# Unit steps in order with values by row tiles, projections in the turned tokens' place, the last diagonal ahead of its index search

## The chip, the cores and the metric

The kernel runs on one core of a Trainium2 chip. Times are device microseconds from the first to the last work of one execution. The engines have these names in the profile: PE is TensorE (PEld its weight loads), DVE VectorE, ACT ScalarE, POOL GpSimd, SP SyncE, whose queue issues most DMA transfers. L12 means line 12 of the kernel before.

## The reference

The block is a "macaron": half an expert layer, attention, half an expert layer, each on a normalised input and added to it. x has 8 batches of 1024 tokens of 512 values; there are 32 experts, each takes 8 tokens of a batch.

```python
def ffn(x):                                   # _layernorm(x) goes in
    logits = einsum('bsd,ed->bse', x, gate_w) + gate_b
    probs = softmax(logits, axis=-2)          # over the tokens
    vals, idx = top_k(probs by expert, 8)
    tok = x[idx];  merged = sum_k(tok * vals) # one mixed token per expert and batch
    h = gelu([merged, 1] @ w1[e]);  o = [h, 1] @ w2[e]
    return scatter_add(o * vals at idx)
def attn(x):                                  # 16 heads of 32
    q, k, v = split_heads(x @ Wq.T + bq), ...
    q = exp(q);  k = exp(k)
    kv = cumsum(k[:, :, :, None] * v[:, :, None, :], axis=1);  k1 = cumsum(k, axis=1)
    out = einsum('zsD,zsDd->zsd', q, kv) / sum(q * k1)
    return merge(out) @ Wo.T + bo
x = x + 0.5 * ffn(layernorm(x))
x = x + attn(layernorm(x))
x = x + 0.5 * ffn(layernorm(x))
```

## The kernel before

The work has four stretches.

**Prologue (0 to about 130 us).** For each batch `gate` (L1335 on) loads and normalises x, turns the tokens (rT, from the pool `rp` of four buffers) and multiplies them with the gate weights; `finish` scales the logits. `choose` (L398 on) takes the eight largest of each expert with MAX8, MATCH_REPLACE8 and FIND_INDEX8; `gather_four` (L431) multiplies the chosen weights with the tokens of four batches (ps_pmT, ps_m). Meanwhile SP's queue loads the first tiles of expert weights (w<-in_w, 2 MB each, named w1_i_e_n and w2_i_e_n). When the pools of the prologue close, new pools are opened on the right side of memory for the projections, and `load_projections` (L200) loads wo, wq, wk and wv, 1 MB each. From wo come ps_bo (L1431), the turned wo (ps_woT) and its product with the gate weights (ps_woG).

**First experts (to about 828 us).** `experts` multiplies each expert's weights with the mixed tokens (h_ps L1206, p_ps L1229). Since this waits for the weights, `speculate` (L1074) runs between: for batches 4 to 7 it computes the q, k and v projections of the input before the expert layer was added and writes them to memory (`ahead_d`), without the scale of the normalisation.

**Attention (to about 1960 us).** Eight batches, each in 8 chunks of 128 tokens; two chunks make a unit (U=2). The loop over b and c (L983 to L1061) gives the order of PE by hand, and the scheduler places what is not pinned (`keep_in_program_order`) on the other engines by its own costs. A chunk runs: `scores` (sp L766, then the mask: am0 on DVE L777, am1 on ACT L782 and selects on POOL L784), in an even chunk `denominators` (ps_den L728, its reciprocal rd L736), then a step of the generator `ahead` (which prepares the next unit), `turn_keys` (ps_kt L816, kc), `project_out` of the chunk before (ps_o L880, addition to xt L887), in an even chunk `spread_denominators` (ps_rr L747), a step of `gate` (the second gate, routed batch by batch) and `attend` (ps_n L830 and L842, at L851, the running sum ps_kv L862 to kv). `begin` adds the first expert layer's result to a later batch's tokens (`scatter_two`, ps_sc L293 and L300, xt L308).

For batches 0 to 3 the generator is `project`. For batches 4 to 7 it is `project_rest` (L619), in steps that `yield` separates. In an even chunk: bo is added to xt (POOL L631), the token scales are spread (ps_rs L636, rsb), pmr (POOL L646) is the routing weight times scale, and pre, the loaded projections, is multiplied by the scale (POOL L650, two halves). In an odd chunk, behind project_out: ps_qk (L663) adds the expert layer's part as a product of pmr and oW; un is its sum with pre (two additions on DVE, L672), and eight exps on ACT (L675); `sum_keys` runs the scan over the keys on DVE (L709, four groups of heads og); ps_v (L684), for each chunk of the unit a product of pmr with oWv, and va (DVE L688); `times_keys` multiplies q and k1 on POOL (qk L720), which the next unit's ps_den reads. pmr holds the same 32 rows four times over (pm4); both ps_v products read the same rows r, those of the batch.

**Last gate and second experts (to the end).** The last batch's gate is done in parts of 4, 2, 1 and 1 chunks (`route` L486). Its last part: the token scales are turned (ps_rsT L378), copied to rsT by ACT (L380), spread (ps_rs L387), the logits scaled, then `choose`, pinned in order with FIND_INDEX8 last (L427), then diag (L512), ps_pmT (L519), pmT, ps_m (L539) and ps_mT (L562). SP waits for ps_m before it can load a next weight tile, as the memory is shared.

Of the kernel before, what the change touches and what calls it, by code (L numbers as in the profile page):

```python
# [15 lines left out]
P = 128  # L16
# [4 lines left out]
def kernel(  # L21
# [188 lines left out]
    def open_token_pools(stack: ExitStack, attention: bool, early=None, keep=None) -> Token:  # L210
        t = Token()
        if attention:


            t.un = keep.enter_context(tc.tile_pool(name="un", bufs=1))
            t.xp = keep.enter_context(tc.tile_pool(name="xp", bufs=1, reuse_waits="tile"))
            t.a1 = stack.enter_context(tc.tile_pool(name="a1", bufs=1))
            t.a2 = stack.enter_context(tc.tile_pool(name="a2", bufs=2))
            t.ow = stack.enter_context(tc.tile_pool(name="ow", bufs=1))
            t.n2 = early.enter_context(tc.tile_pool(name="n2", bufs=2, side="right"))  # L220
        if not attention:
# [150 lines left out]
    def gate_scale(t, s, b, lg, rs, at, k):  # L372
# [6 lines left out]
        rsT = t.p2.tile([NCH, P], F32, tag="rsT", name=f"rsT_{b}_{at}")  # L379
        nc.scalar.copy(rsT[:k, :], pr[:k, :])  # L380
        yield
# [21 lines left out]
    def choose(t, lg, rows, g, name, listed=False, el=None):  # L403
# [21 lines left out]
        if pinned:  # L425
            tc.keep_in_program_order(
                nc.vector.max_index(chosen_idx[rows, g, :], top[rows, :], lg[rows, :])  # L427
            )
        return rest, sm[rows, 2:3]
# [51 lines left out]
    def route(t, s, b, el=None):  # L481
# [30 lines left out]
        nc.vector.tensor_scalar_mul(diag[rows, :], ident[rows, rows], r)  # L512
        if el is None:
# [105 lines left out]
    def project_rest(t, s, b, u):  # L619

        xt, mv, rs = s["xt", b]
        pre = s.pop(("pre", b, u))
# [30 lines left out]
        yield  # L653
        yield

# [17 lines left out]
        for n, bias in ((1, bk_sb), (0, bq_sb)):  # L673
            for oc in range(NDC):
                nc.scalar.activation(  # L675
                    qkT[:, oc, n, :], qkT[:, oc, n, :], AF.Exp, bias=bias[:, oc : oc + 1]
                )
        sum_keys(t, s, b, u)

        r = slice(32 * (b % 4), 32 * (b % 4) + E)  # L680
        for i in range(U):
            c = u * U + i
            ps = t.mm.tile([P, D], F32, tag="mm", name=f"ps_v_{b}_{c}")
            nc.tensor.matmul(  # L684
                ps, lhsT=pmr[r, i * P : (i + 1) * P], rhs=s["oWv"][r, :], start=True, stop=True
            )
            va = t.a2.tile([P, D], F32, tag="va", bufs=3, name=f"va_{b}_{c}")
            nc.vector.scalar_tensor_tensor(  # L688
                va,
                pre[:, (2 * NDC + i * 2) * UT : (2 * NDC + i * 2 + 2) * UT],  # L690
                rs[:, c : c + 1],
                ps,
                ALU.mult,
                ALU.add,
            )
            s["va", b, c] = va
        times_keys(t, s, b, u)
        yield

# [4 lines left out]

    def sum_keys(t, s, b, u):
        k1 = s["k1", b, u]
        before = s.pop(("k1", b, u - 1), None)
        for og in range(NDC):
            nc.vector.tensor_tensor_scan(  # L709
                k1[:, og, :],  # L710
                ones.to_broadcast([P, UT]),
                s["k", b, u][:, og, :],
                0.0 if before is None else before[:, og, UT - 1 : UT],
                ALU.mult,
                ALU.add,
            )

    def times_keys(t, s, b, u):
        qk = t.a1.tile([P, NDC, UT], F32, tag="qk", name=f"qk_{b}_{u}")
        nc.gpsimd.tensor_mul(qk, s["q", b, u], s["k1", b, u])  # L720
        s["qk", b, u] = qk
# [189 lines left out]
    def outputs_ahead(t, s):  # L911
# [4 lines left out]
        for i in range(2):  # L916
# [13 lines left out]
            evacuate(s["oW"][:, 2 * i : 2 * i + 2], ps)  # L930
        s["oWv"] = t.ow.tile([P, D], F32, name="oWv")
# [5 lines left out]
        evacuate(s["oWv"], ps)  # L937

    def attention(t, early, preload):
# [47 lines left out]
        for b in range(B):  # L987
            for c in range(NCH):
                if c == 0:
# [15 lines left out]
                if c > 1:  # L1005
                    next(begun, None)
                if b == B - 1 and c == 1:
                    preload(0)
                if b == B - 1 and c == NCH - 2:
# [6 lines left out]
                    )  # L1016
                    gate = route(t, s, b, el)
                scores(t, s, b, c)
                if c % U == 0:
                    denominators(t, s, b, c // U)  # L1020
                    nb, nu = divmod(b * (NCH // U) + c // U + 1, NCH // U)
                    if (nb, nu) == (NB0, 0):
# [9 lines left out]
                        )  # L1032
                        load_ahead(t, s, nb, nu)
                    if (nb, nu) > (0, 1):
                        of = project if nb < NB0 else project_rest
# [255 lines left out]
    with ExitStack() as stack:  # L1291
        big = stack.enter_context(tc.tile_pool(name="big0", bufs=1))
        with ExitStack() as inner:
# [10 lines left out]
            ]  # L1304
            t = open_token_pools(inner, False)
            (
# [322 lines left out]
```

## Time and profile before

| what | value |
|---|---|
| median of 3 runs | 2622.33 us (2621.52 to 2624.72) |
| the profiled execution | 2632.39 us, its span 2630.6 us |
| PE busy, share | 2192.9 us, 83% |
| DVE, ACT, POOL busy | 869.0, 500.2, 376.7 us |
| DMA moved | 667.98 MB, 254 GB/s over the span |
| mean granted clock of TensorE | 0.910 |
| 830 to 1495 us (batches 0 to 3) | PE 648.33 of 665 us, clock 0.99, 30 GB/s |
| 1515.8 to 1631 us (batch 4) | PE 104.93 of 115.2 us, clock 0.88 |
| 1631 to 1747 us (batch 5) | PE 101.83 of 116 us, clock 0.91 |
| 1747 to 1863 us (batch 6) | PE 104.15 of 116 us, clock 0.85 |
| 1863 to 1961 us (batch 7) | PE 87.79 of 98 us, clock 0.95 |

The page's second part shows the span in 40 equal slices: a digit is the busy share in tenths (9 is 90% or more), PEclk the clock granted to TensorE in tenths of full speed, DMA the busy share of the 16 DMA engines. A line of waits says which operation of an engine waited for which operation of another, how long in all, how often, and the longest. A timeline line gives start, duration, engine, line and operation, and in square brackets the idle time before it with what ended it. Granted clock 0.5 means that matmuls take twice the time, which a busy share does not show.

### The profile page before, as it was taken

How to read it: one execution, taken by the hardware profiler on the slowest of the kernel's cores; microseconds unless marked ns; L12 is line 12 of the kernel's file. 1: busy time of each engine (PE TensorE's matmuls, PEld its weight loads, DVE VectorE, ACT ScalarE, POOL GpSimd, SP SyncE). 2: the span in 40 equal slices, each digit the busy share in tenths (PEclk: the TensorE clock that was granted, in tenths of full speed). 3: DMA queues.
4: the chain of work that ended last, by engine and by line, in shares of the span. 5: the costliest groups of instructions: out<-in, count | busy, mean ns of one | idle time of the engine just before them, and what ended most of it. 6: DMA issues, size and time to landing. Idle time of an engine off the chain costs nothing.

```text
span 2630.6 us, 41801 instructions
## 1 busy us (share of the span) xinstructions
PE 2192.9 (83%) x18679; PEld 1161.7 (44%) x18679; DVE 869.0 (33%) x1493; ACT 500.2 (19%) x967; POOL 376.7 (14%) x345
## 2 busy tenths in 40 slices
PE   8699999998986999999999989898886656656555
PEld 5354445444533666666666655555541111111111
DVE  7311111111101443444535476767651000100002
ACT  6310000000000322222222243343430000000000
POOL 0000000000000212111122244444324000000002
PEclk9899999999997999999999988988997787777887
DMA  7699999999996000010100323323149999999995
GB/s 275 253 427 426 428 427 427 426 427 427 428 429 255 1 17 1 21 49 19 58 2 19 91 86 129 118 99 107 66 175 377 423 427 428 428 428 428 428 428 248
DMA packets 95477, 667.98 MB, mean 254 GB/s; under 512 B 18222, under 2 KB 22574, under 8 KB 58432
## 3 DMA queue, kind: packets, MB, share of 16 engines
q1 hardware_dynamic: 73792, 621.45, 57.4%
q10 hardware_dynamic: 18432, 35.66, 3.5%
q0 software_dynamic: 3072, 8.19, 0.8%
q8 instruction: 147, 2.41, 0.4%
q14 instruction: 34, 0.28, 0.0%
HBM read 614.34 MB, written 48.23 MB: 252 GB/s over the span
## 4 chain that ended last, share of the span: by engine, by line
PE 49%; issue 22%; DMA 18%; DVE 7%; ACT 3%; POOL 1%; SPq 0%; ACTq 0%; POOLq 0%; DVEq 0%
DMA w<-in_w 13%; PE ps_o L880 8%; PE ps_k L599 4%; PE ps_q L599 4%; PE ps_v L800 4%; PE ps_sk L1116 3%; PE ps_sq L1116 2%; PE p_ps L1229 2%; PE ps_n L830 2%; PE sp L766 2%; PE h_ps L1206 2%; PE ps_sv L1133 2%; PE ps_n L842 2%; DMA pg<-pmT_d,chosen_idx 1%; DVE st L314 1%
## 5 line engine op out<-in xcount | busy, mean ns | idle before, releaser
L1206 PE MATMUL h_ps<-w,mT 128*8 128x512 f32 x2048 | 287.1, 696 | 120.3 <-DMA w<-in_w 118.3
L1229 PE MATMUL p_ps<-w,pm 128*32 128x512 f32 x1024 | 177.9, 830 | 137.3 <-DMA w<-in_w 133.9
L1215 DVE STREAM_TRANSPOSE hs<-h_ps 128x512 f32<-128x512 f32 x64 | 45.9, 717 | 719.2 <-PE h_ps L1206 719.2
L880 PE MATMUL ps_o<-wo_sb,at 128*128 128x512 f32 x512 | 240.0, 613 | 0.9 <-DVE at L851 0.8
L1206 PEld LDWEIGHTS h_ps<-w,mT 128*8 128x8 f32 x2048 | 50.9, 95 | 338.2 <-issue 206.9
L1229 PE MATMUL p_ps<-w,gl 128*32 128x512 f32 x1024 | 135.1, 658 | 41.9 <-DMA w<-in_w 40.0
L590 POOL TENSOR_TENSOR xt<-xt,bo_sb 128x512 f32<-128x512 f32 x32 | 45.8, 1446 | 798.0 <-PE ps_ocT L338 737.9
L1229 PEld LDWEIGHTS p_ps<-w,pm 128*32 128x32 f32 x1024 | 35.7, 132 | 276.6 <-issue 130.8
L880 PEld LDWEIGHTS ps_o<-wo_sb,at 128*128 128x128 f32 x512 | 96.2, 198 | 101.9 <-issue 98.1
L784 POOL TENSOR_SCALAR_AFFINE_SELECT am<-am 128x512 f32<-128x512 f32 x128 | 78.7, 639 | 414.3 <-ACT am L782 272.3
L314 DVE BATCH_NORM_STATS2 st<-xt 128x6 f32<-128x512 f32 x192 | 129.3, 685 | 4.9 <-DMA xt<-in_x 2.0
L599 PE MATMUL ps_k<-xnT,wk_sb 128*128 128x256 f32 x512 | 115.3, 383 | 10.8 <-ACT xnT L339 10.8
L1222 ACT ACTIVATE pm<-a 128x128 f32<-128x128 f32 x32 | 9.9, 309 | 588.5 <-DVE a L1217 588.5
L1116 PE MATMUL ps_sq<-xcT,wq_sb 128*128 128x256 f32 x512 | 117.9, 387 | 4.0 <-ACT xcT L241 4.0
L1116 PE MATMUL ps_sk<-xcT,wk_sb 128*128 128x256 f32 x512 | 117.1, 385 | 0.0
L1133 PE MATMUL ps_sv<-wv_sb,xcT 128*128 128x512 f32 x256 | 115.6, 599 | 0.0
L800 PE MATMUL ps_v<-wv_sb,xnT 128*128 128x512 f32 x256 | 115.1, 593 | 0.0
L599 PE MATMUL ps_q<-xnT,wq_sb 128*128 128x256 f32 x512 | 115.1, 383 | 0.0
L1116 PEld LDWEIGHTS ps_sq<-xcT,wq_sb 128*128 128x128 f32 x512 | 96.4, 192 | 34.7 <-issue 17.2
L1116 PEld LDWEIGHTS ps_sk<-xcT,wk_sb 128*128 128x128 f32 x512 | 96.9, 192 | 28.4 <-issue 16.2
L599 PEld LDWEIGHTS ps_k<-xnT,wk_sb 128*128 128x128 f32 x512 | 96.0, 190 | 28.2 <-ACT xnT L339 14.6
L766 PE MATMUL sp<-un 32*128 32x128 f32 x2048 | 101.9, 296 | 7.2 <-ACT un L675 6.9
(245 smaller groups left out, 2901.2 us busy)
## 6 DMA issues: line engine op xcount, KB each, us to landing
w<-in_w SPq DMA_DIRECT2D x256, 2048.0 KB, 29.9
xt<-in_x SPq DMA_DIRECT2D x31, 1024.0 KB, 10.1
pre<-ahead_d SPq DMA_DIRECT2D x16, 1536.0 KB, 6.9
ahead_d<-ahead_qk ACTq DMA_DIRECT2D x16, 1024.0 KB, 11.5
out<-xt SPq DMA_DIRECT2D x16, 1024.0 KB, 4.4
xs<-in_x ACTq DMA_DIRECT2D x16, 512.0 KB, 18.1
ahead_d<-ahead_v ACTq DMA_DIRECT2D x16, 512.0 KB, 10.9
pm<-pm SPq DMA_DIRECT2D x16, 128.0 KB, 2.4
```

Of the source, the lines that this page charges most:

```text
L314: nc.vector.bn_stats(st, xt[:, c, :])
L599: nc.tensor.matmul(ps[:, o, :], lhsT=w_sb[n][:, dc, oc * P : (oc + 1) * P], rhs=xnT[:, dc, :], start=(dc == 0), stop=(dc == NDC - 1),)
L766: nc.tensor.matmul(sp[r // 2][:, r % 2, og, :], lhsT=kT[hr, og, cols], rhs=qT[hr, og, cols], start=True, stop=True,)
L784: nc.gpsimd.affine_select(out=am[1][:, i, :, :], in_=am[1][:, i, :, :], pattern=[[0, NDC], [1, P]], compare_op=ALU.is_ge, fill=0.0, base=0 ...
L800: nc.tensor.matmul(ps, lhsT=s["xnT", b, c // U][:, dc, cols], rhs=w_sb["v"][:, dc, :], start=(dc == 0), stop=(dc == NDC - 1),)
L830: nc.tensor.matmul(ps[hr, og, :], lhsT=va[:, (og * HG + r) * HD : (og * HG + r + 1) * HD], rhs=am[r // 2][:, r % 2, og, :], start=(og == 0 ...
L842: nc.tensor.matmul(ps[hr, og, :], lhsT=kv[hr, og, :], rhs=qT[hr, og, cols], start=False, stop=True, skip_group_check=True,)
L880: nc.tensor.matmul(ps, lhsT=at[:, oc, :], rhs=w_sb["o"][:, oc, :], start=(oc == 0), stop=(oc == NDC - 1),)
L1116: nc.tensor.matmul(ps[:, o, :], lhsT=w_sb[w][:, dc, oc * P : (oc + 1) * P], rhs=xcT[:, dc, :], start=(dc == 0), stop=(dc == NDC - 1),)
L1133: nc.tensor.matmul(ps, lhsT=xcT[:, dc, i * P : (i + 1) * P], rhs=w_sb["v"][:, dc, :], start=(dc == 0), stop=(dc == NDC - 1),)
L1206: nc.tensor.matmul(h[32 * j : 32 * j + B, :], lhsT=mT[:, dc, e, :], rhs=w1h[dc // 2][:, dc % 2, j * 512 : (j + 1) * 512], start=(dc == 0), ...
L1229: nc.tensor.matmul(pp[32 * j : 32 * (j + 1), :], lhsT=gl4[e % 4][:, q, :, :].rearrange("p i b -> p (i b)"), rhs=w2h[q // (NU // 2)][:, q % ...
```

## The change

It has three parts.

1. *Projections.* The pool `rp` moves to the right side of memory, in an ExitStack of its own (`turned`) that closes after the last `gate` is issued. The pools for wo and for wq, wk and wv are opened there, with waits by tile, and their loads are issued before `finish` of the last two batches and the second `gather_four`. On SP's queue they come after w1_0_0_0 and w1_0_0_1; before, they came after w1_0_0_0, w1_0_0_1, w1_0_1_0, w1_0_1_1 and w2_0_0_0. On PE, ps_bo, ps_woT and ps_woG come ahead of the first expert's matmuls.
2. *Unit steps.* For batches 4 to 7 the even chunk ends with ps_qk, the additions and the exps, behind `attend`. The odd chunk begins with `turn_keys`, the pair of ps_v with va, and the gate's step; then come `scores`, `project_out` of the chunk before, `sum_keys` and `times_keys`, and `attend`. The step of `begin` comes later in the odd chunk. The two ps_v of a unit read two different groups of 32 rows of pmr and of two copies of oWv (`oWv` 0 and 1), the second made by two transfers once. The scan of group 0 and the product on POOL are pinned: on DVE that scan comes behind at of the odd chunk, the other three before am0 of it.
3. *Last gate.* Where one chunk is scaled (k == 1), DVE copies rsT instead of ACT. In the last batch diag is made ahead of FIND_INDEX8.

```diff
-            t.rp = stack.enter_context(tc.tile_pool(name="rp", bufs=4))
+            t.rp = early.enter_context(tc.tile_pool(name="rp", bufs=4, side="right"))
...
-        nc.scalar.copy(rsT[:k, :], pr[:k, :])
+        (nc.vector.tensor_copy if k == 1 else nc.scalar.copy)(rsT[:k, :], pr[:k, :])
...
         if pinned:
-            tc.keep_in_program_order(
-                nc.vector.max_index(chosen_idx[rows, g, :], top[rows, :], lg[rows, :])
-            )
+            return rest, sm[rows, 2:3], top
...
-        chosen, r = choose(t, lg, rows, g, f"b{b}", True, el)
+        chosen, r, *top = choose(t, lg, rows, g, f"b{b}", True, el)
         diag = t.p2.tile([P, E], F32, tag="diag", name=f"diag_{b}")
-        nc.vector.tensor_scalar_mul(diag[rows, :], ident[rows, rows], r)
+        scaled = nc.vector.tensor_scalar_mul(diag[rows, :], ident[rows, rows], r)
+        if el is not None:
+            tc.keep_in_program_order(scaled)
+            tc.keep_in_program_order(
+                nc.vector.max_index(chosen_idx[rows, g, :], top[0][rows, :], lg[rows, :])
+            )
...
     def project_rest(t, s, b, u):
...
             load_ahead(t, s, *divmod(b * (NCH // U) + u + 1, NCH // U))
-        yield
         yield
...
-        sum_keys(t, s, b, u)
-
-        r = slice(32 * (b % 4), 32 * (b % 4) + E)
+        yield
+
+        ps = [t.mm.tile([P, D], F32, tag="mm", name=f"ps_v_{b}_{u * U + i}") for i in range(U)]
+        for i in range(U):
+            r = slice(E * ((b + i) % 4), E * ((b + i) % 4 + 1))
+            nc.tensor.matmul(
+                ps[i],
+                lhsT=pmr[r, i * P : (i + 1) * P],
+                rhs=s["oWv", i][r, :],
+                start=True,
+                stop=True,
+            )
         for i in range(U):
             c = u * U + i
-            ps = t.mm.tile([P, D], F32, tag="mm", name=f"ps_v_{b}_{c}")
-            nc.tensor.matmul(
-                ps, lhsT=pmr[r, i * P : (i + 1) * P], rhs=s["oWv"][r, :], start=True, stop=True
-            )
...
-        times_keys(t, s, b, u)
+        yield
+
+        sum_keys(t, s, b, u, True)
+        times_keys(t, s, b, u, True)
         yield
...
+            if pinned and og == 0:
+                tc.keep_in_program_order(scan)
...
-        nc.gpsimd.tensor_mul(qk, s["q", b, u], s["k1", b, u])
+        product = nc.gpsimd.tensor_mul(qk, s["q", b, u], s["k1", b, u])
+        if pinned:
+            tc.keep_in_program_order(product)
...
+                rest = NB0 <= nb < B
+                if c > 1 and not (rest and c % U):
                     next(begun, None)
...
+                if rest and c % U:
+                    turn_keys(t, s, b, c)
+                    next(ahead)
+                    next(gate, None)
                 scores(t, s, b, c)
...
+                        oWv = s["oWv", 1] = t.s1.tile([P, D], F32, name="oWv1")
+                        nc.sync.dma_start(oWv[E:], s["oWv", 0][: 3 * E])
+                        nc.sync.dma_start(oWv[:E], s["oWv", 0][3 * E :])
...
-                else:
+                elif not rest:
                     next(ahead, None)
...
-                turn_keys(t, s, b, c)
+                if not (rest and c % U):
+                    turn_keys(t, s, b, c)
...
                 else:
+                    if rest and c > 1:
+                        next(begun, None)
                     next(ahead, None)
-                next(gate, None)
+                if not (rest and c % U):
+                    next(gate, None)
...
                 attend(t, s, b, c)
+                if rest and c % U == 0:
+                    next(ahead)
...
+            wo, early = ExitStack(), ExitStack()
             for b in range(B):
                 gate(b)
+                if b == B - 1:
+                    turned.close()
+                    load_projections(
+                        wo.enter_context(
+                            tc.tile_pool(name="wo", bufs=1, side="right", reuse_waits="tile")
+                        ),
+                        "o",
+                    )
+                    load_projections(
+                        early.enter_context(
+                            tc.tile_pool(name="wqkv", bufs=1, side="right", reuse_waits="tile")
+                        ),
+                        "qkv",
+                    )
                 if b:
                     finish(b - 1)
...
-        wo = ExitStack()
-        load_projections(wo.enter_context(tc.tile_pool(name="wo", bufs=1, side="right")), "o")
-        early = ExitStack()
-        load_projections(early.enter_context(tc.tile_pool(name="wqkv", bufs=1, side="right")), "qkv")
```

More of the change, by code (lines that the diff above doesn't have):

```diff
@@ L691, in project_rest @@
                 rs[:, c : c + 1],
-                ps,
+                ps[i],
                 ALU.mult,
@@ L703, in load_ahead, with sum_keys @@
         s["pre", b, u] = pre
-    def sum_keys(t, s, b, u):
+    def sum_keys(t, s, b, u, pinned=False):
         k1 = s["k1", b, u]
@@ L708, in sum_keys @@
         for og in range(NDC):
-            nc.vector.tensor_tensor_scan(
+            scan = nc.vector.tensor_tensor_scan(
                 k1[:, og, :],
@@ L716, in sum_keys, with times_keys @@
             )
-    def times_keys(t, s, b, u):
+            if pinned and og == 0:
+                tc.keep_in_program_order(scan)
+    def times_keys(t, s, b, u, pinned=False):
         qk = t.a1.tile([P, NDC, UT], F32, tag="qk", name=f"qk_{b}_{u}")
-        nc.gpsimd.tensor_mul(qk, s["q", b, u], s["k1", b, u])
+        product = nc.gpsimd.tensor_mul(qk, s["q", b, u], s["k1", b, u])
+        if pinned:
+            tc.keep_in_program_order(product)
         s["qk", b, u] = qk
@@ L930, in outputs_ahead @@
             evacuate(s["oW"][:, 2 * i : 2 * i + 2], ps)
-        s["oWv"] = t.ow.tile([P, D], F32, name="oWv")
+        s["oWv", 0] = t.ow.tile([P, D], F32, name="oWv")
         ps = t.mm.tile([P, D], F32, tag="mm", name="ps_oWv")
@@ L936, in outputs_ahead @@
             )
-        evacuate(s["oWv"], ps)
+        evacuate(s["oWv", 0], ps)
     def attention(t, early, preload):
@@ L1004, in attention @@
                         begun = begin(b + 1)
-                if c > 1:
+                nb, nu = divmod(b * (NCH // U) + c // U + 1, NCH // U)
+                rest = NB0 <= nb < B
+                if c > 1 and not (rest and c % U):
                     next(begun, None)
@@ L1020, in attention @@
                     denominators(t, s, b, c // U)
-                    nb, nu = divmod(b * (NCH // U) + c // U + 1, NCH // U)
                     if (nb, nu) == (NB0, 0):
@@ L1033, in attention @@
                         load_ahead(t, s, nb, nu)
+                        oWv = s["oWv", 1] = t.s1.tile([P, D], F32, name="oWv1")
+                        nc.sync.dma_start(oWv[E:], s["oWv", 0][: 3 * E])
+                        nc.sync.dma_start(oWv[:E], s["oWv", 0][3 * E :])
                     if (nb, nu) > (0, 1):
-                        of = project if nb < NB0 else project_rest
+                        of = project_rest if rest else project
                         ahead = of(t, s, nb, nu) if nb < B else iter(())
                         next(ahead, None)
-                else:
+                elif not rest:
                     next(ahead, None)
@@ L1304 @@
             ]
-            t = open_token_pools(inner, False)
+            turned = ExitStack()
+            t = open_token_pools(inner, False, turned)
             (
```

## The prediction

> **What bounds the kernel now.** I begin with the page's rows over 40 slices, because the kernel is a sequence of stages and an average over all of them describes none.
>
> ```profile
> PE   8699999998986999999999989898886656656555
> PEclk9899999999997999999999988988997787777887
> DMA  7699999999996000010100323323149999999995
> GB/s 275 253 427 426 428 427 427 426 427 427 428 429 255 1 17 1 21 49 19 58 2 19 91 86 129 118 99 107 66 175 377 423 427 428 428 428 428 428 428 248
> ```
>
> A slice is 65.8 us. Slices 3 to 12 (the first expert stage, to about 828 us) and the last ten (the second) run the DMA at 426 to 429 GB/s with nothing to spare: there, only when the weight stream starts decides. In slices 13 to 22 TensorE is busy at full clock (attention of batches 0 to 3; the change leaves their order alone). In slices 23 to 29 (attention of batches 4 to 7, 1515 to 1961 us) neither is full and the clock sinks. Slices 1 and 2 hold the prologue. So there are three places: the start of the first stream, batches 4 to 7, and the start of the second stream.
>
> Place one, in stretches of 5 us (columns: busy time of PE, PEld, DVE, ACT, POOL, granted clock, DMA share, GB/s), and the chain that ended last:
>
> ```profile
> 100.00:105.00 5.00, 4.34 (x28) 2.31 (x32) 2.63 (x5) 0.00 (x0) 0.00 (x0) 0.62 0.45 192
> 105.00:110.00 5.00, 5.00 (x52) 1.22 (x44) 0.00 (x0) 0.00 (x0) 0.00 (x0) 1.00 0.00 0
> 110.00:115.00 5.00, 1.62 (x12) 0.57 (x12) 2.76 (x7) 1.12 (x2) 0.00 (x0) 0.91 0.81 269
> 115.00:120.00 5.00, 5.00 (x40) 1.12 (x36) 0.42 (x1) 0.00 (x0) 0.00 (x0) 0.75 0.96 383
> ```
>
> ```profile
> 112.93 12.16 DMA wo_sb<-in_woT
> 125.33 6.55 PE ps_bo L1431 x8
> ```
>
> The DMA empties its queue near 102 us and stands still until the last gathers have run and the pools of the prologue close.
>
> Place two, the waits of PE between 1515 and 1965 us (total, times, longest), and its timeline at two units:
>
> ```profile
> PE ps_den L728 <- POOL qk L720: 17.1, 8, 2.8
> PE ps_n L830 <- DVE va L688: 12.9, 12, 1.6
> PE sp L766 <- ACT un L675: 6.9, 11, 1.0
> ```
>
> ```profile
> 1743.45 1.08 PE L728 MATMUL ps_den<-qk,hsum 128*32 128x256 f32 x8 [2.80 <-POOL qk L720]
> ...
> 1761.10 0.59 PE L684 MATMUL ps_v<-oWv,pmr 32*128 32x512 f32 x1
> ...
> 1761.95 1.02 PE L684 MATMUL ps_v<-oWv,pmr 32*128 32x512 f32 x2
> ...
> 1782.25 0.69 PE L293 MATMUL ps_sc<-o_all,pm 32*128 32x512 f32 x1
> 1782.73 0.69 PE L300 MATMUL ps_sc<-odd 32*128 32x512 f32 x1
> ...
> 1783.32 1.42 PE L766 MATMUL sp<-un 32*128 32x128 f32 x27
> ```
>
> The stage is a loop through all engines, with waits of 1 to 3 us, and no engine is saturated (PE .88 of the time, DVE some .68).
>
> Place three, the last gate before the second stream:
>
> ```profile
> 1969.79 0.24 ACT L380 COPY rsT<-ps_rsT 1x128 f32<-1x128 f32 x1
> 1975.32 1.22 DVE L427 FIND_INDEX8 chosen_idx<-top_b,lg 32x8 uint32<-32x1024 f32 x1
> 1976.73 3.62 PE L519 MATMUL ps_pmT<-diag,pm 32*128 32x32 f32 x16 [6.25 <-DVE diag L512]
> ```
>
> **The change, part by part.** The working is against the profiled execution, 2632.39 us (span 2630.6 and 1.8 around it). The runs' median is 2622.33, 0.4% lower; the differences are taken over unchanged.
>
> *Projections.* The four projection loads (4.2 MB) now wait only for the turned tokens of the last gates (last read by PE at 91.7 us) and stand on SP's queue after two weight tiles instead of seven. Idle DMA between 100 and 115 us is 5 × (.55 + 1.00 + .19) = 8.7 us, and 115 to 120 adds some .2: about 9. Afterwards two tiles (to about 92), the projections at the 385 GB/s of the rows (11 us, to about 103) and the remaining tiles follow without a gap. Is the 9 us passed on? The stream is full to 828 us, and PE waits for w there for 49.8 us in 28 waits, so it can take the data 9 us earlier. What is behind the moved loads on SP's queue are five weight tiles that PE first needs after 113 us; they land by about 127, and the first expert's matmuls now come behind ps_bo and the turned wo on PE, so nothing is late. Should wv be held up until finish(7) (94 us), the queue stops for 2 us. −9, between −7 and −9.5.
>
> *Last gate.* rsT is copied by DVE instead of ACT. On ACT it had waited from 1968.9 (ps_rsT's end) for a table load and junk until 1969.79; on an idle DVE it runs at once: −0.9. FIND_INDEX8 with its value load (1.28 us) goes behind diag: −1.3. It is then covered by ps_pmT (3.62) and would cost 1.3 without that cover; the gathers that need its index start 12 us later (1988.35). The weights of the stream's next tile, whose memory waits for ps_m, come earlier by the sum: −2.2, between −1 and −2.5.
>
> *Entry to batch 4.* The first unit's order begins one chunk early. Scores and ps_o of batch 3 used to fill PE while POOL made pre twice and pmr (to 1515.8); now they sit behind ps_qk, so 1.17 + 3.70 of PE work follows that wait. Part hides in the next chunk's waits: +2, between 0 and +4. The two added oWv1 transfers (64 KB by count, under 1 us by the lines of like size) are ahead of pm4's on SP, behind which POOL works until 1515.1: nothing.
>
> *Units of batches 4 to 7* (16, about 111 us per batch).
> (a) ps_v: four passes in sequence take 1.87 us from the first start to the last end. Here the Trainium skill has a rule, in "TensorE: Matmul & The Clock Gate", "Part 3: Packing small matmuls": operations in different row tiles run at the same time, some 4 ns apart, which would halve the 1.87 to 0.93. The row nearest, ps_sc, is the same shape in two row tiles, and starts its second .48 us after the first; the next stream begins 1.07 us after the first start. By the rule 16 × .94 = 15 us, by the row 16 × .8 = 12.8, both only if PE is what the loop waits for. I take the row.
> (b) va is ready before the scores: the 12.9 us of ps_n<-va go. The exps no longer stand between ps_o and the next even chunk, so the 6.9 of sp<-un go in their present place.
> (c) In exchange the pinned scan of group 0 stands behind at of the odd chunk on DVE, and POOL's qk behind it. An example, batch 5's second unit, counted from the end of ps_o of its even chunk: DVE's order holds xt, st, two additions of ps_sc, two more st and two aggregates (6 × .69 + 2 × .18 = 4.5), at .69, an aggregate .18 and the scan .67: 6.0. POOL's product takes 2.36: 8.4. PE meanwhile waits .7 for xt, then ps_n 2.0, ps_kv .4, ps_sc 1.0 and the next sp 1.1: 5.2. ps_den waits the rest, 3.2. Counted so, the four units of a batch wait 3.2, 3.5, 4.1 and 1.3 us (before 17.1 / 4 = 4.3 together). Behind ps_den on PE are held ps_rs, ps_kt and ps_o, 1.1 + 3.5 us that don't need it; DVE's rd and POOL's pre wait for them. Further, sp(odd) waits about 1.9 a unit for the two additions of un (2 × 1.22), with the gate product and ps_o queued behind.
> (d) The same hand count for the two orders gives, at full clock, 103.5 us a batch before and 104.8 after, while PE's own work falls from 89.5 to 86. Measured before: 116.8. The 13 us between are half-clock stretches.
>
> Those stretches decide. Columns as above:
>
> ```profile
> 1742.00:1749.00 7.00, 5.55 (x20) 3.19 (x21) 3.01 (x3) 2.24 (x3) 5.40 (x5) 0.52 0.60 225
> 1766.00:1776.00 10.00, 10.00 (x102) 7.63 (x97) 8.78 (x17) 4.94 (x10) 5.45 (x5) 0.51 0.49 172
> ```
>
> After 2.8 us of idle PE the clock is halved for 7 us, after 1.6 us (1763.2 to 1764.85) for 10, about one stretch a unit. The skill's rule on this ("TensorE: Matmul & The Clock Gate", "Part 1: The HAM clock gate") speaks against the change: it takes an idle window of about 3.4 us to halve the clock, and ps_den's waits are to grow past that in three of four units. By the rule alone the 2.8 and 1.6 would cost nothing and twelve of the new waits one half-clock window each, 12 × 1.7 = +20 us. By the rows such stretches are there already at shorter waits, and the ones after ps_n<-va should go with their cause while those after ps_den stay: from −8 to +8 a batch. I take the rows, and the middle: 0 for the stage, since what (d) adds (1.3 × 4 = +5) is what one lost stretch of 7 to 10 us (3.5 to 5 us) gives back.
>
> Sum: −9 − 2.2 + 2 + 0 = −9 us: 2623 of the profiled execution, 2613 of the median.
>
> **Rivals.**
> A, likeliest, .48: as above; stage between −5 and +5: 2606 to 2618.
> B, .20: the row tiles and the vanished waits shorten the loop too. For it: 12.9 + 6.9 us of waits named above have no cause left, and PE's work is 3.5 a batch less. Against it: the wait on POOL's qk stays. −4 to −8 a batch, 2581 to 2600.
> C, the other side, .25: ps_den's wait on POOL's qk. It speaks for it that three of four counted waits exceed the longest seen so far; against it, that PE has 3.5 us a batch less to do. If the wait is 3.5 to 4 us a unit and each brings a further half-clock stretch of 7 us (3.5 us lost), the stage gains 16 × 1.5 = 24 us at most and keeps 10 on average. It decides from +9 for the stage (.6 a unit), where the front's gain is used up. 2622 to 2645, mostly 2628 to 2638.
> D, .07: the change doesn't do at the front what it says: wo waits for a late release of the pool, or the stream's gain meets a PE that isn't ready. 7 to 9 us come back: 2617 to 2625.
>
> **How the numbers follow.** The time is A's, 2613. What a measurement can't tell from no change is .2%, 5.2 us: 2617.1 to 2627.6. Faster: all of B, .44 of A, none of C and .02 of D = .66. Same: .04 of A, .04 of C, .05 of D = .13. Slower: .21 of C. The range leaves out the lower half of B and the upper part of C: 2588 to 2637; A's own is 2606 to 2618.
>
> **What would show it.** Right: no 5 us stretch between 85 and 130 us with a DMA share under .8; the end of the first stream some 9 us earlier; FIND_INDEX8 beside ps_pmT; no wait ps_n<-va; ps_v's second start under .5 us after its first. Wrong: waits of ps_den over 4 us with more stretches at half clock (C), or a mean clock above .93 between 1515 and 1961 (B). The likeliest error is in the middle value 0 of the stage, which rests on clock stretches that no count of instructions gives.

## The result, and the profile after

The changed kernel takes 2656.48 us (median of 4 runs, 2653.33 to 2658.27); before takes 2621.95 us (4 runs, 2621.52 to 2624.72). The ratio is 1.0127, 95% interval 1.0115 to 1.0139: some 34 us slower, where 2613 (2588 to 2637) was forecast. The sign and the range were both wrong. The profiled execution of the change took 2658.27 us, its span 2656.6.

The rows over 40 slices of the changed kernel (a slice is now 66.4 us):

```profile
PE   8799999998977999999999888888896655555555
PEclk9899999999988999999999988888897787778787
DMA  7799999999994000010100323313139999999995
GB/s 273 312 423 427 428 426 427 426 427 427 428 429 153 1 17 17 5 49 19 59 17 8 129 76 112 131 68 106 65 142 372 421 429 427 429 427 429 427 429 246
```

The first weight stream moves more in slice 2 (312 against 253 GB/s) and less in slice 13 (153 against 255): it starts and ends earlier. In slices 24 to 29, most of batches 4 to 7, the clock is at 8 tenths throughout; before it was at 8 or 9. In stretches of 5 us (PE, PEld, DVE, ACT, POOL, granted clock, DMA share, GB/s), and SP's own queue:

```profile
100.00:105.00 5.00, 2.89 (x16) 1.93 (x20) 2.90 (x5) 0.71 (x2) 0.00 (x0) 0.50 1.09 419
105.00:110.00 5.00, 5.00 (x48) 1.31 (x44) 0.44 (x1) 0.00 (x0) 0.00 (x0) 0.87 1.01 429
110.00:115.00 5.00, 2.83 (x28) 0.79 (x19) 1.78 (x4) 0.00 (x0) 0.00 (x0) 1.00 0.97 397
```

```profile
82.31 0.51 SPq L204 DMA_DIRECT2D wo_sb<-in_woT  x1
82.86 0.74 SPq L204 DMA_DIRECT2D wq_sb<-in_wqT  x1
93.32 0.37 SPq L204 DMA_DIRECT2D wk_sb<-in_wkT  x1
```

The gap of the DMA is closed: no stretch of 5 us between 85 and 130 us has a share under .97. wk (not wv, as the prediction had it) waits until 93.3 us for memory that the last gates' ps_lg reads, but the transfers issued ahead of it keep the DMA busy. After the first stream the same operation (ps_ocT) starts at 822.54 us and before at 830.52: 8.0 us gained, and still there when batch 3 ends. The waits of PE from batch 4 on (those between 1493 and 1994 us; in all, how often, the longest):

```profile
PE ps_den L744 <- POOL qk L734: 46.6, 16, 4.4
PE ps_qk L667 <- POOL pmr L651: 7.2, 1, 7.2
PE ps_rs L388 <- DVE va L697: 5.2, 4, 1.3
PE ps_mT L566 <- DVE va L697: 5.2, 4, 1.3
PE ps_pmT L523 <- DVE va L697: 5.2, 4, 1.3
PE sp L782 <- DVE un L676: 3.8, 7, 0.6
```

Here is the wait that grew most. ps_n no longer waits for va, but the gate's products ps_rs, ps_mT and ps_pmT do (15.6 us together), and ps_den waits 46.6 us against 17.1. That is the prediction's sign for its rival C: waits over 4 us with more stretches at half clock. One unit of batch 5, on PE, DVE and POOL:

```profile
1733.31 1.17 PE L782 MATMUL sp<-un 32*128 32x128 f32 x32
1738.83 1.08 PE L744 MATMUL ps_den<-qk,hsum 128*32 128x256 f32 x8 [4.35 <-POOL qk L734]
```

```profile
1733.82 0.66 DVE L867 TENSOR_TENSOR at<-ps_n,un 128x512 f32<-128x512 f32 x1
...
1735.37 0.20 DVE L987 RECIPROCAL rs<-sd 128x8 f32<-128x8 f32 x1 [0.80 <-ACT sd L986]
1735.49 0.86 DVE L721 TENSOR_TENSOR_SCAN un<-ones,un,un 128x256 f32<-128x256 f32 x1
```

```profile
1736.43 2.35 POOL L734 TENSOR_TENSOR qk<-un 128x1024 f32<-128x1024 f32 x1 [0.63 <-DVE un L721]
```

The one pinned scan of head group 0 starts at 1735.49, behind at and here behind a wait of DVE for ACT as well; POOL can't begin before it, and PE doesn't pass ps_den: ps_rs, which doesn't need it, starts at 1739.85, behind it. The last gate, for the lines shown of before:

```profile
1995.42 0.28 DVE L381 COPY rsT<-ps_rsT 1x128 f32<-1x128 f32 x1 [0.45 <-PE ps_rsT L378]
...
2001.28 1.22 DVE L515 FIND_INDEX8 chosen_idx<-top_b,lg 32x8 uint32<-32x1024 f32 x1
2001.35 3.62 PE L523 MATMUL ps_pmT<-diag,pm 32*128 32x32 f32 x16 [5.18 <-DVE diag L511]
```

From the last xt to ps_pmT it is now 8.54 us (1992.81 to 2001.35), before 10.32.

### The profile page after: what moved, and what is told of

It is laid out like the page before. It is cut to its first block, busy times and chain, and to the rows that moved or that the text cites. A ratio compares the mean times of both kernels' runs of the same rounds, so it can differ in the third digit from the quotient of the medians.

```text
span 2656.6 us, 41783 instructions
## 1 busy us (share of the span) xinstructions
PE 2197.0 (83%) x18679; PEld 1160.3 (44%) x18679; DVE 865.9 (33%) x1495; ACT 500.2 (19%) x965; POOL 381.2 (14%) x345
## 4 chain that ended last, share of the span: by engine, by line
PE 50%; issue 23%; DMA 14%; DVE 4%; POOL 3%; ACT 2%; SPq 0%; POOLq 0%; ACTq 0%; DVEq 0%
DMA w<-in_w 10%; PE ps_o L896 9%; PE ps_k L603 4%; PE ps_q L603 4%; PE ps_v L816 4%; PE ps_sq L1148 3%; PE ps_sk L1148 3%; PE h_ps L1238 3%; PE p_ps L1261 3%; DMA xg<-out,chosen_idx 2%; PE ps_sv L1165 2%; PE sp L782 2%; PE ps_n L846 2%; POOL qk L734 2%; PE ps_n L858 2%
## 5 line engine op out<-in xcount | busy, mean ns | idle before, releaser
L1261 PE MATMUL p_ps<-w,pm 128*32 128x512 f32 x1024 | 172.4, 806 | 138.9 <-DMA w<-in_w 132.2
L896 PE MATMUL ps_o<-wo_sb,at 128*128 128x512 f32 x512 | 259.8, 655 | 0.1
L896 PEld LDWEIGHTS ps_o<-wo_sb,at 128*128 128x128 f32 x512 | 103.9, 214 | 114.3 <-issue 110.5
L1165 PE MATMUL ps_sv<-wv_sb,xcT 128*128 128x512 f32 x256 | 115.6, 599 | 0.0
```

The costliest lines, as they stand in the source:

```text
L896: nc.tensor.matmul(ps, lhsT=at[:, oc, :], rhs=w_sb["o"][:, oc, :], start=(oc == 0), stop=(oc == NDC - 1),)
L1165: nc.tensor.matmul(ps, lhsT=xcT[:, dc, i * P : (i + 1) * P], rhs=w_sb["v"][:, dc, :], start=(dc == 0), stop=(dc == NDC - 1),)
L1261: nc.tensor.matmul(pp[32 * j : 32 * (j + 1), :], lhsT=gl4[e % 4][:, q, :, :].rearrange("p i b -> p (i b)"), rhs=w2h[q // (NU // 2)][:, q % ...
```

## The experiments

The time of batches 4 to 7 is read between stores of x on SP's queue that every kernel has. The first part, the entry, still holds the last unit of batch 3; the last store ends batch 7. The table gives the length of each part, PE's busy and idle time in all of it, and the mean granted clock. The profiled execution of before lay 10 us above its median. The second row has the same unit code and shows the stage at 490; by the ratios of their runs the change is 44 us slower than it, and the table has 43.7.

| kernel | entry | batch 4 | 5 | 6 | 7 | sum | PE busy | PE idle | clock |
|---|---|---|---|---|---|---|---|---|---|
| before | 63.6 | 112.7 | 108.1 | 116.1 | 99.0 | 499.5 | 450.0 | 49.5 | 0.91 |
| projections alone | 63.1 | 109.3 | 109.0 | 109.6 | 99.2 | 490.2 | 442.2 | 48.0 | 0.93 |
| the change | 70.4 | 121.7 | 119.2 | 116.2 | 106.4 | 533.9 | 457.4 | 76.5 | 0.89 |
| change, kept warm | 70.2 | 116.1 | 115.6 | 115.5 | 105.2 | 522.6 | 468.3 | 54.3 | 0.92 |
| change, scan not pinned | 68.2 | 103.0 | 101.9 | 102.9 | 98.1 | 474.1 | 440.0 | 34.1 | 0.93 |

All ratios below are against runs of the kernel before on the same chip, with their 95% intervals.

**1. The projections alone** (the hunks on `rp`, `turned` and load_projections, nothing else).

```diff
-            t.rp = stack.enter_context(tc.tile_pool(name="rp", bufs=4))
+            t.rp = early.enter_context(tc.tile_pool(name="rp", bufs=4, side="right"))
```

> The kernel before with the move of the projections alone. The trace of the whole change shows the first weight stream about 8 us ahead at the start of attention. Theory one (the loss is all in the units of batches 4 to 7): 2614, 8 us under before. Rival (the front pays later, because the second stream or a queue of the DMA shifts): 2620 to 2623.

2614.92 us, 0.9958 (0.9933 to 0.9982): 11 us gained, 5 to 18, as theory one had it. The gain reaches the end.

**2. The last gate alone** (rsT by DVE, diag ahead of the index search).

```diff
-        nc.scalar.copy(rsT[:k, :], pr[:k, :])
+        (nc.vector.tensor_copy if k == 1 else nc.scalar.copy)(rsT[:k, :], pr[:k, :])
```

> The kernel before with the last gate's two edits alone (rsT by DVE, diag ahead of the index search). By the prediction's sum 2.2 us under before: 2620. By the trace of the whole change, where only 0.4 us of it is left at the end, because the weight stream and not the gate ends last: 2621 to 2622.

2626.3 us, 1.0007 (0.9995 to 1.0018): no gain that can be measured, and the 2.2 us of the prediction lie outside the interval. The path from the last xt to ps_pmT is shorter in its trace too (8.53 us), and the end isn't.

**3. The units alone** (order and row tiles, projections and last gate as before).

```diff
+                if rest and c % U == 0:
+                    next(ahead)
```

> The new order of the units with the row tiles alone; projections and last gate as before. Theory one (everything lost is lost here): 2622 + 34.5 + 8 + 1 = 2665, between 2660 and 2668. Rival (parts of the loss come from the three edits together): under 2658.

2665.06 us, 1.0143 (1.0115 to 1.0171). The three parts multiply to 1.0108, against 1.0127 for the change, which their intervals allow. The loss is in the units, the entry to batch 4 included.

**4. Kept warm.** Nine more matmuls in the ten units with the long wait; ps_den overwrites what they write.

```diff
         ps = t.mm.tile([P, UT], F32, tag="mm", name=f"ps_den_{b}_{u}")
+        for _ in range(9 if b >= NB0 and u and (b, u) < (B - 1, 2) else 0):
+            nc.tensor.matmul(ps[:, :P], lhsT=ident, rhs=ident, start=True, stop=True)
```

> The whole change, and nine more matmuls of the identity into ps_den's own bank ahead of ps_den in the ten units in which it waits 3.2 to 4.4 us for POOL's product (each pair 0.64 us at full clock, 2.9 us in all, so they end before the product does). ps_den overwrites them. Theory two (what costs is the clock that is halved after a wait of over 3 us): the ten waits no longer halve it, ps_den's eight passes take 0.64 instead of 1.08 us, and 10 stretches of about 2 us are saved: 2630 to 2642. Rival (what costs is the wait itself, and everything queued behind it): no gain, 2655 to 2660.

2647.99 us, 1.0079 (1.0054 to 1.0104) against the change's 1.0127: 8.5 us by the medians, 13 by the ratios, which is between the two theories. The timeline of PE in batch 4, first of the change, then of this kernel at the same wait:

```profile
1551.94 1.08 PE L744 MATMUL ps_den<-qk,hsum 128*32 128x256 f32 x8 [3.54 <-POOL qk L734]
```

```profile
1545.92 2.27 PE L744 MATMUL ps_den<-ident 128*128 128x128 f32 x18
1549.54 0.64 PE L746 MATMUL ps_den<-qk,hsum 128*32 128x256 f32 x8 [1.34 <-POOL qk L734]
```

With the wait cut from 3.54 to 1.34 us by work that is of no use, ps_den runs at full clock (0.64 instead of 1.08 us). It does so at nine of the ten. PE busy without the 22.8 us of added matmuls is 445.5, against 457.4: PE's own matmuls take 11.9 us less, and the stage is 11.3 us shorter. So the halved clock behind these ten waits is a real cost, shown. The waits themselves remain, and so do other stretches of half clock (below).

**5. The product early.**

```diff
             s["va", b, c] = va
+        sum_keys(t, s, b, u)
+        times_keys(t, s, b, u, True)
         yield
-
-        sum_keys(t, s, b, u, True)
-        times_keys(t, s, b, u, True)
         yield
```

> The whole change, but the scans and POOL's product stand in the step of ps_v and va, ahead of the odd chunk's scores, instead of behind project_out with the scan of group 0 pinned behind at. Theory three (the loss is the loop at -> scan -> product -> ps_den): ps_den no longer waits (46.6 us in the change), the half-clock stretches behind it go too, and the time falls by 25 to 40 us: 2616 to 2632. Rival (POOL's selects of am1 now stand behind the product, 2.4 us, and ps_n of the odd chunk waits in its place): a gain under 12 us, 2645 to 2656.

2608.85 us, 0.9930 (0.9914 to 0.9947), faster than the 2616 to 2632 expected. ps_den waits no more (its list of waits has no such line), and the change, with nothing else altered, is faster than before. The rival's price is there and small: ps_n waits for POOL's selects in twelve places, 3.1 us in all.

**6. No row tiles, in the change.**

```diff
-            r = slice(E * ((b + i) % 4), E * ((b + i) % 4 + 1))
+            r = slice(E * (b % 4), E * (b % 4 + 1))
...
-                rhs=s["oWv", i][r, :],
+                rhs=s["oWv", 0][r, :],
```

> The whole change, but both products ps_v of a unit read the same 32 rows and one oWv, as before. If the row tiles gain what the prediction's row gave (12.8 us): 2669. If ps_v is covered by the wait of ps_den behind it, as the loop decides and not PE: 2654 to 2660.

The second copy of oWv isn't made then either. 2662.3 us, 1.0133 (1.0116 to 1.0150): not to be told from the change. ps_v takes 33.0 us on PE instead of 18.5, and the gate's waits for va fall from 15.6 to 7.2. Over the stage PE is busy for 470.8 us instead of 457.4 and idle for 66.8 instead of 76.5: of the 13.4 us that the row tiles save on PE, 9.7 come back as idle time.

**7. The projections and the row tiles, in the old order** (the first experiment, and the pair of ps_v with oWv1).

```diff
-            r = slice(32 * (b % 4), 32 * (b % 4) + E)
+            r = slice(E * ((b + i) % 4), E * ((b + i) % 4 + 1))
```

> The kernel before with the move of the projections and the row tiles for ps_v, in the old order of the unit steps. The projections alone gave 0.9958 of the time before. If PE's work is on the path in the old order: 0.8 us a unit more, 12.8 in all, 2600 to 2604. If it is not (va on DVE ends the wait of ps_n): 2610 to 2616.

2617.66 us, 0.9966 (0.9955 to 0.9977), where the projections alone gave 0.9958. Again nothing. The first two lines are waits and the last a group, all of this kernel:

```profile
PE ps_n L835 <- DVE va L693: 19.8, 12, 2.5
PE ps_den L733 <- POOL qk L725: 18.2, 9, 2.8
```

```profile
L683 PE MATMUL ps_v<-oWv,pmr 32*128 32x512 f32 x64 | 16.9, 604 | 0.0
```

ps_v fell from 31.6 to 16.9 us, and ps_n's wait for va rose from 12.9 to 19.8: half of the gain is seen to turn into waiting for DVE's va. (The profiled execution, at 2629.46, was the slowest of nine.)

**8. The same, kept warm** at the six old waits of 2.4 to 2.8 us.

```diff
+        for _ in range(6 if (b, u) in ((4, 3), (5, 0), (6, 0), (6, 3), (7, 0), (7, 3)) else 0):
+            nc.tensor.matmul(ps[:, :P], lhsT=ident, rhs=ident, start=True, stop=True)
```

> The same as the run with the projections and the row tiles, with six matmuls of the identity ahead of ps_den in the six units where ps_den waited 2.4 to 2.8 us before (1.9 us at full clock). Theory two (these waits halve the clock for 7 us each, 3.5 us lost): 6 x 2 to 3.5 = 12 to 20 us less than without. Rival (waits under 3 us don't halve it; the stretches have another cause): within 3 us of it.

2612.72 us, 0.9953 (0.9937 to 0.9969). The intervals overlap: inconclusive, and short of 12 us. The waits of ps_den fall from 18.2 to 7.4 us, and the clock over the stage, 0.93, is that of the projections alone, where nothing was filled. That waits below 3 us are what the old order's half clock hangs on, as the prediction read its rows, isn't shown.

**9. The scan not pinned.** One word of the change.

```diff
-        sum_keys(t, s, b, u, True)
+        sum_keys(t, s, b, u)
```

> The whole change, one word less: the scan of head group 0 isn't pinned, so the scheduler puts it ahead of am0 of the odd chunk, with the other three, and POOL's product comes right behind the selects of am1 and ahead of the two additions of bo. Nothing moves on PE. Theory three (the pinned scan behind at, and the product that waits for it, is the loss): 2610 to 2622, near the run with the product early (0.993). Rival (the place of the product in the step of the values matters, or the selects and additions on POOL): 2635 to 2656.

2594.58 us, 0.9886 (0.9867 to 0.9906), better than expected: 30 us faster than before, and some 62 faster than the change. DVE and POOL in a unit of batch 5 now:

```profile
1692.00 2.65 DVE L721 TENSOR_TENSOR_SCAN un<-ones,un,un 128x256 f32<-128x256 f32 x4
1694.57 1.20 DVE L793 TENSOR_TENSOR am<-sp,mask 128x1024 f32<-128x1024 f32 x1
```

```profile
1696.07 2.34 POOL L734 TENSOR_TENSOR qk<-un 128x1024 f32<-128x1024 f32 x1
1701.47 2.50 POOL L636 TENSOR_TENSOR xt<-xt,bo_sb 128x512 f32<-128x512 f32 x2 [3.06 <-DVE st L314]
```

```profile
1701.48 1.17 PE L782 MATMUL sp<-un 32*128 32x128 f32 x32
1702.58 0.64 PE L744 MATMUL ps_den<-qk,hsum 128*32 128x256 f32 x8
```

All four scans run together, POOL's product begins in the time of ps_o and is ready 4 us before ps_den wants it. There is no wait line for ps_den in the whole stage. Why the fifth kernel, which makes the product early too, stays 11 us behind this one isn't worked out; its stage takes 488.0 us at a clock of 0.91.

**10 to 12. More on top of the early product.** The first unit of batch 4 in its old place (10), project_out first in the odd chunk (11), both (12).

```diff
+                late_first = (nb, nu) == (NB0, 0)
+                ahead_now = rest and not late_first
```

> The run with the scans and the product early, but the first unit of batch 4 takes its steps in the odd chunk, behind project_out, as before. There PE waited 6.6 us for pmr with nothing behind it, against 2.3 before. If the entry costs what the traces show (6 us): 2600 to 2605. If the next chunks take it up: 2607 to 2611.

```diff
-                if rest and c % U:
+                moved = rest and c % U and last is not None
+                if moved:
+                    project_out(t, s, *last)
+                scores(t, s, b, c)
+                if moved:
                     turn_keys(t, s, b, c)
                     next(ahead)
                     next(gate, None)
-                scores(t, s, b, c)
```

> The run with the scans and the product early, but in the odd chunk project_out of the even one comes first, then scores, turn_keys, ps_v and the gate's step. ps_o (3.5 us at full array) then covers the two additions of un and nothing waits for va (15.6 + 3.8 us of waits there), and the stretch of small matmuls is split in two. If these waits and the half clock behind them are on the path: 20 to 30 us less, 2580 to 2590. If am0 and the selects then end the wait of ps_n: within 5 us of 2609.

> Both edits, the first unit late and project_out first. The sum of the two gains; if each is real, 6 us under the faster one.

2603.57 us (0.9911, 0.9891 to 0.9932), 2601.01 us (0.9910, 0.9891 to 0.9929) and 2594.65 us (0.9881, 0.9862 to 0.9900), against 0.9930 for the fifth. Each single step overlaps with it; only both together are clear, and they are 6 us under the faster one, as expected. The 11th was expected 20 to 30 us faster and missed: the waits for va and un fell from 19.4 to 7.3 us, and others came in their place (three of PE's waits in that kernel):

```profile
PE ps_o L895 <- DVE at L866: 8.9, 5, 3.0
PE ps_n L845 <- DVE am L792: 6.3, 4, 1.8
PE ps_n L845 <- DVE va L697: 5.1, 5, 1.1
```

**13 and 14. On top of the unpinned scan:** the first unit late (as in 10), and no row tiles (as in 6).

> The whole change with the scan of group 0 not pinned (0.9886), and the first unit of batch 4 in the odd chunk behind project_out. With the product early that edit took 5 us. If the entry's cost stands on its own: 2588 to 2591. If the unpinned scan's order takes it up: 2593 to 2596.

> The whole change with the scan not pinned, and both ps_v from the same 32 rows. In the change itself and in the old order the row tiles moved the time by less than can be told (PE's 14.5 us went into longer waits for va). If with ps_den's wait gone PE's work is on the path: 13 us more than unpinned, 2604 to 2610. If va still absorbs it: 2593 to 2600.

2599.02 us (0.9894, 0.9876 to 0.9913) and 2596.43 us (0.9878, 0.9856 to 0.9900), against 0.9886. Neither edit can be told from none; the first came out above both of its expectations (up to 2596). The change without its pin beats both kernels, and no gain from the row tiles is seen in it: without them PE is busy for 451.1 us instead of 440.0 and idle for 25.7 instead of 34.1.

## Why the prediction was wrong

The units of batches 4 to 7 were put at 0. The table sets the terms of that 0, and of the entry, against the traces, with either profile of the old unit code (us):

| term | forecast | before to change | projections alone to change |
|---|---|---|---|
| entry | +2 | +6.8 | +7.3 |
| batches 4 to 7, PE idle | +19 | +20.1 | +21.1 |
| batches 4 to 7, PE busy | −19 | +7.5 | +15.3 |
| sum | +2 | +34.4 | +43.7 |

The forecasts of idle and busy time follow from (d): per batch 103.5 and 104.8 us, with 89.5 and 86 of them PE's own work, so idle time grows from 14.0 to 18.8 and work falls by 3.5, four times; the clock was to give back another 5.

**Projections: right.** −9 was forecast (−7 to −9.5); the traces show −8.0 at the end of the stream, the run alone −11 (−5 to −18). PE's waits for weights there are still 49.0 us (49.8 before): the stage is bound by the stream and moved forward as a whole.

**Last gate: the path right, its worth not.** −2.2 forecast; ps_pmT came 1.8 us sooner, the end 0.4 (26.4 us late at the last store of x, 26.0 at the end), and alone it gave nothing. ps_mT ran for 1.90 us instead of 1.06, at half clock, which takes back 0.84 of it. The remaining half microsecond isn't traced.

**Entry to batch 4: mis-sized.** +2 forecast (0 to 4); the traces show 70.4 us where before had 63.6, nearly 7. PE stands 7.2 us for pmr (2.3 before) with nothing behind it, and the work that used to fill that time follows it in full; little of it hid in later waits. In the time of a run the edit that mends it is within the noise (10, 13), so this is shown by traces alone.

**Units (a): the size right, by luck; the worth wrong.** ps_v fell by 13.1 us (31.6 to 18.5; 12.8 forecast). But the row of ps_sc from which the 12.8 was read, with starts 0.48 us apart, is an exception: at ten of its twelve places in that trace the two start within 0.01 us. So they do in the change, and the pairs of ps_v start within 0.02 us of each other, nearer to the rule that (a) set aside than to its row. The four passes take 1.13 us in most units, where the row gave 1.07 and the rule 0.93:

```profile
1718.31 1.13 PE L687 MATMUL ps_v<-oWv,pmr 32*128 32x512 f32 x4
...
1729.85 0.69 PE L293 MATMUL ps_sc<-o_all,pm 32*128 32x512 f32 x1
1729.86 0.69 PE L300 MATMUL ps_sc<-odd 32*128 32x512 f32 x1
```

No gain in time is seen in three orders (6, 7, 14): most of what PE saves comes back as idle time. (a) itself said that the gain counts only if PE is what the loop waits for.

**Units (b): half right.** The wait of ps_n for va went, but waits for va did not: 12.9 us before, 15.6 at the gate's products now. By the code these take a buffer from the pool of three (`mm`) of which the pair of ps_v holds two until va has read it, and the waits end as the first va does.

**Units (c) and the idle time of (d): right.** The waits of ps_den were forecast as 3.2, 3.5, 4.1 and 1.3 us in the units of a batch, 48 in all; those of batch 4 measure 3.3, 3.5, 4.3 and 1.6, and all together 46.6. sp's new waits were overrated (30 forecast, 19.4 with the gate's). The waits named in (b) and (c), added up, are +42 (+31, +30, −12.9, −6.9), twice what came; the chain followed by hand through the units gave +19 and was right to 2 us, with some luck, as sp's part of it was too high. The 116.8 us a batch that (d) calls measured stands in no trace; the table of before has 115.2, 116 and 116 for batches 4 to 6.

**The clock: here it failed.** PE's matmuls were to take 19 us less and take 7 to 15 more. The step that failed is the middle, 0, of −8 to +8 us a batch, with one lost stretch giving back 5 us. It rests on the sentence that the stretches after ps_n<-va go with their cause while those after ps_den stay. In the trace of the change both are there. By the clock records of the trace, twenty-four stretches of the stage, 3.4 to 10.2 us each, run at half clock: ten at ps_den's waits of 3.2 us and more, and ten that begin within 3.1 us after one of the twelve waits for va, which only moved. One of each (first and third line; columns as above), and the wait for va in the third:

```profile
1552.00:1558.00 6.00, 6.00 (x21) 3.39 (x22) 3.96 (x7) 0.96 (x2) 6.00 (x6) 0.58 0.00 0
1558.00:1566.00 8.00, 7.50 (x134) 4.41 (x132) 4.54 (x7) 2.35 (x6) 2.82 (x2) 1.00 0.01 2
1566.00:1573.00 7.00, 6.21 (x48) 5.47 (x49) 4.90 (x8) 4.13 (x9) 1.05 (x2) 0.59 0.63 223
```

```profile
1566.79 2.58 PE L523 MATMUL ps_pmT<-diag,pm 32*128 32x32 f32 x13 [1.29 <-DVE va L697]
```

By the mean clock over the stage, half clock covers about 90 us in before's profile (2 × (1 − 0.91) × 499.5), 69 in that of the projections alone and 117 in the change's. The passes of ps_v start 0.85 us apart in such a stretch of before's trace and 0.43 outside, so half of what is added is lost: an estimate of 14 to 24 us, where the forecast had 5 us less. The rest, some 5 to 8 us by which PE's own work didn't fall as far as 14, isn't assigned. Much of the half clock falls on the large products; ps_o, the same 280 matmuls, before and after:

```profile
L880 PE MATMUL ps_o<-wo_sb,at 128*128 128x512 f32 x280 | 135.6, 630 | 0.9 <-DVE at L851 0.8
L896 PE MATMUL ps_o<-wo_sb,at 128*128 128x512 f32 x280 | 155.4, 706 | 0.1
```

The Trainium skill's rule ("TensorE: Matmul & The Clock Gate", "Part 1: The HAM clock gate"), an idle window of about 3.4 us, had given +20 in the prediction's own working. For ps_den it agrees: all ten waits of 3.2 us and more are followed by ps_den at half clock (1.08 us), all six of 1.3 to 1.6 by ps_den at full (0.64), and the fourth experiment took 11.9 us of it away. For va it doesn't: by the rule waits of 1.3 us cost nothing. In the unpinned kernel (9), where ps_den waits no more, all twelve of them still have such a stretch behind them:

```profile
1690.66 1.08 PE L566 MATMUL ps_mT<-isum,m 128*128 128x32 f32 x8 [1.30 <-DVE va L697]
```

```profile
1691.80:1695.20 3.40, 3.40 (x32) 2.39 (x33) 3.40 (x6) 1.83 (x3) 0.32 (x1) 0.50 1.07 386
```

Without row tiles (14) these waits are only 0.4 to 1.0 us, and eleven of the twelve have one. So idle time alone doesn't halve the clock there. What does stays open; the small matmuls of 32 rows around these waits may count for little activity, but no run here separates that.

**Rivals.** C named the place and the mechanism, ps_den's wait with half clock behind it. Its price (+24 at most for the stage, 2645 at most in all) was too low: batches 4 to 7 alone took 28 to 36 us more. B's number is what the change gives without the pin (0.9886 of 2622 is 2592), but not by B's reasons: the wait on POOL's qk, which B left standing, is the one that is gone (17.1 us before), the waits for va are still 15.6 us, and the row tiles aren't needed (14). Of the 59.8 us of the stage between the change and its unpinned form (533.9 and 474.1), 42.4 are idle PE and 17.4 longer matmuls. A allowed 5 us either way for a stage whose clock the working itself left open by 8 us a batch, 32 in all; the 14 to 24 us lie within that width.

## What to carry to other kernels

Forecast an engine's idle time and its busy time as two terms: here the first was right to 2 us and the second, which held the clock, had the wrong sign. Where a rule and the rows price one term with different signs, the middle is no forecast; the whole width goes into the range. Before a wait is counted as gone, look at what else needs the same buffer: the waits for va only changed their owner. An instruction pinned on one engine is read with the next two engines: the scan is 0.7 us of DVE, but POOL's product and TensorE's queue stood behind it. A saving on an engine that isn't the last to finish is spent on the next wait, and in this kernel each wait of TensorE of over 3 us in the units had its half-clock stretch on top.

## What was not expected of the hardware

Matmuls of no use, placed in a wait, made the kernel faster: 2.27 us of identity products ahead of ps_den in ten units gave 8.5 us by the medians and 13 by the ratios, as the clock was not halved at nine of these waits. The clock was halved all the same in stretches where PE waited for no more than 0.4 to 1.3 us. And the same unit code took 499.5 us in one profiled execution and 490.2 in another, with PE busy 450.0 and 442.2 us for the same instructions: 7.8 of the 9.3 us are the same matmuls taking longer, so a single profile is no measure of this stage to better than some 2%.
